# A four-layer image kernel: the row spectrum of the third layer stored component, frequency, line

## The chip, the cores and the metric

The kernel runs on one core of one Trainium2 chip. The metric is the device time of one execution in microseconds (us). The kernel before took 8232.35 us, the median of 3 runs (8224.83 to 8241.54). The profile shown below is of one more execution, whose span is 8232.3 us.

## The reference

Four images of 64 x 64 pixels and 128 channels pass through four residual layers, x = x + layer(groupnorm(x)), all in float32. The change lies in the third, a Fourier attention layer in which each of the 128 channels is one token, an image of 64 lines by 64 columns. Cut to what the changed code computes:

```python
# _L2_conv_ref: 128 tokens per image, 16 heads
tokens_norm = instance_norm(tokens)
k, q = fno_layer(tokens_norm, ..., (32, 32)), fno_layer(tokens_norm, ..., (32, 32))
v    = fno_layer(tokens_norm, ..., (64, 64))
attn = softmax(q @ k.T / scale) @ v                    # over the tokens, per head
attn = instance_norm(fno_layer(attn, proj_w, ...) + tokens)
m = gelu(fno_layer(instance_norm(attn), mixer_w1, ..., norm=...))
m = fno_layer(m, mixer_w2, ..., norm=...)
out = instance_norm(m) + attn

# fno_layer: resampled 1x1 convolution + spectral_conv, which is
xft = rfftn(x); out_ft[low modes] = xft[low modes] * w; irfftn(out_ft)
```

The layer has one channel in and one out per token, so a spectral weight is one complex number per mode. The Gram product of all tokens over their low modes stands for the scores of the convolution with a scalar part.

## The kernel before

The layers run one after the other. The first is a selective scan and takes most of the span; the third begins at about 6600 us and ends at about 7660 us of the profile; the fourth, windowed attention, takes the rest.

The third layer is `layer2_image`, a generator that is run once for each of the four images. `layer2` lets two images run interleaved: `Pace` keeps a model clock of each engine and `in_turn` advances the image that is due next, so the order of the instructions on TensorE (PE), VectorE (DVE), ScalarE (ACT) and GpSimd (POOL) is fixed when the program is built, and each engine works its list off in that order. All instructions are recorded in `Pace`'s helper, so the profile gives line L884 for nearly all of the layer; they are told apart by the names of their tiles. Images 0 and 1 form the first pair, 2 and 3 the second.

An image lies in SBUF as 32 tiles of 128 partitions, each tile holding two lines of the token images. The parts that the change or the prediction touches, in the order of an image:

- `token_stats` and the norm: DVE statistics `in_st`, matmuls `in_pm`, the scale `n_sc` on ACT and DVE, the selectors `so`, matmuls `pc`.
- `dft_y` transforms each line of 64 columns into 32 frequencies of two components. Eight groups of four matmuls write `pu` in PSUM (4 tiles of 128 values: line, component, frequency), and one ACT copy for each group brings 8 lines into `U`, which is `[128, 64 lines, 2 components, 32 frequencies]`. `dft_y` is called three times per image: once at the start on `xg`, and once in each of the two calls of `spectral`.
- The column transform of the first call, matmuls `px`: for each of 32 frequencies and 2 components, the 64 lines of one frequency are the stationary operand, `U[:, :, q, 4 * g + e]`, and the 68 columns of `quad` are moved. Four frequencies share a PSUM tile and are copied by ACT into `Xs`. GpSimd copies corners of `Xs` into `XG`, whose transposes are `pT`.
- The Gram product: `pv` (stationary `gram`, moved `U` for 8, 7 or 1 frequencies by 64 lines) goes by an ACT copy into a tile `V`, and then for each frequency a matmul `pG` takes the 66 x 64 slice `V_last[0][:, :, e]` as its stationary and as its moving operand.
- After `pT`, DVE copies `TT` and DVE and GpSimd build the three-part `Z`; the scores `psc` need it. Softmax on DVE and ACT (`Sc`), transposes `pp`, the combined matrix `BI`, and matmuls `pk`, whose result goes to HBM and back (`ti`, `z`).
- `pz`: for both images of the pair, products `WX` on DVE and GpSimd are the stationary operand, 68 contiguous columns, and 64 contiguous columns of `PT` are moved; ACT copies the result into `Zp`.
- `synthesis` (matmuls `pa`, `pb`), norms, and twice `spectral`: there four matmul groups `pq` move `U` for 16 lines by 32 frequencies over stationary `quad`, and DVE multiplies each result by `mix` into `Zp`.

The PSUM pool has three buffers for each of the tags `a` (`pu`, `pv`, `pT`) and `b` (`px`, `pq`, `pz`). A float32 matmul appears in the profile as two records.

Of the kernel before, what the change touches and what calls it, by code (L numbers as in the profile page):

```python
# [11 lines left out]
F32 = mybir.dt.float32  # L12
AF = mybir.ActivationFunctionType
ALU = mybir.AluOpType
# [3 lines left out]
P = 128  # L18
Q = 68
# [64 lines left out]
def layer0(sh, A, x_in, x_out, scr):  # L84
# [7 lines left out]
    with ExitStack() as ctx:  # L92
# [300 lines left out]
        def products(G, q, hT):  # L393
            U = G["unit"]
            rev = U["rev"]
            qo = 3 - q if rev else q
            e = qo // 2
            if U["yT"][e] is None:
                U["yT"][e] = psy.tile([P, 2, 2 * P], F32, name=f"yT{e}")
                if U["k"] == 0:  # L400
                    for r in range(2):
                        for s in range(2):
                            t0 = (2 * e + r) * P
                            nc.tensor.matmul(
                                U["yT"][e][:, r, s * P : (s + 1) * P],
                                lhsT=U["u"][:, s, t0 : t0 + P],
                                rhs=D_diag[:, s, :],
                                start=(r == 0 and s == 0),
                                stop=False,
                                skip_group_check=True,  # L410
                            )
                    U["started"] |= {(e, j) for j in range(4)}
            for j in range(4):
                jo = 3 - j if rev else j
                nc.tensor.matmul(  # L415
                    U["yT"][e][32 * jo : 32 * jo + 32, qo % 2, :],
                    lhsT=U["Ws"][G["g"]][:, :, 4 * q + j],
                    rhs=hT[:, j, :],
                    start=((e, jo) not in U["started"]),
                    stop=(G["g"] == 3),  # L420
                    skip_group_check=True,
                )
                U["started"].add((e, jo))
            if G["g"] == 3 and q % 2:

                y, k = U["y"], U["k"]
                ye = y[:, 2 * e : 2 * e + 2, :]
                if k == 1:
                    nc.scalar.copy(ye, U["yT"][e])
                else:  # L430
                    nc.vector.tensor_tensor(ye, ye, U["yT"][e], ALU.add)  # L431
                if k == 2:
                    for r in range(2):
                        nc.vector.bn_stats(U["st"][:, 4 * U["pc"] + 2 * e + r, 0, :], y[:, 2 * e + r, :])
                if q == 3:
                    nc.sync.dma_start(U["dst"](k), y)
# [482 lines left out]
def layer2_image(sh, w, pools, x_in, x_out, scr, wt, parity, beside):  # L919
# [4 lines left out]
    nc = sh.nc  # L924
    big, tmp, small, ps = pools
# [3 lines left out]
    tt, ts = nc.vector.tensor_tensor, nc.vector.tensor_scalar  # L929
# [3 lines left out]
    large = lambda name, shape=T: big.tile(shape, F32, name=name, tag="big", bufs=7)  # L933
# [53 lines left out]

    def dft_y(src):

        U = large("U2", [P, 64, 2, 32])  # L990
        for g in range(NJ // 4):
            pu = ps.tile([P, 4, P], F32, name="pu", tag="a")
            for q in range(4):
                nc.tensor.matmul(pu[:, q, :], lhsT=src[:, 4 * g + q, :], rhs=w["an"], start=True, stop=True)
            nc.scalar.copy(U[:, 8 * g : 8 * g + 8].rearrange("p t q r -> p (t q r)"), pu.rearrange("p q m -> p (q m)"))
            yield g == 7
        return U

    def synthesis(Z, put):


        def columns(g0):
            S = tmp.tile([P, 4, 2, P], F32, name="S2", bufs=3)
            for e in range(0, 4, 2):
                pa = ps.tile([P, 2, 256], F32, name="pa", tag="a")
                for q in range(2):
                    g = g0 + e + q
                    nc.tensor.matmul(
                        pa[:, q, :],
                        lhsT=Z[:, 4 * g : 4 * g + 4, :].rearrange("p t r -> p (t r)"),  # L1010
                        rhs=w["sy"],
                        start=True,
                        stop=True,
                    )
                nc.scalar.copy(S[:, e : e + 2].rearrange("p g q c -> p (g q c)"), pa.rearrange("p g m -> p (g m)"))
            return S

        S = columns(0)
        yield False
        for g0 in range(0, 16, 4):  # L1020
            S_next = columns(g0 + 4) if g0 < 12 else None
            for u in range(2):
                pb = ps.tile([P, 4, DM], F32, name="pb", tag="b")
                for q in range(2):
                    nc.tensor.matmul(
                        pb,
                        lhsT=w["bd"][64 * u : 64 * u + 64, q, :],
                        rhs=S[64 * u : 64 * u + 64, :, q, :],
                        start=(q == 0),
                        stop=(q == 1),  # L1030
                    )
                put(u, g0, pb)
            S = S_next
            yield g0 == 12

    def at(t, u, g0):
        return t.rearrange("p (g u) c -> p u g c", u=2)[:, u, g0 : g0 + 4, :]
# [47 lines left out]
    for n in range(2):  # L1085
        nc.tensor.matmul(
            pc[:, n : n + 1],
            lhsT=M2[:, n].rearrange("p a j u -> p (a j u)"),
            rhs=w["ones"][:, 0:1],
            start=True,  # L1090
            stop=True,
# [10 lines left out]
    U = yield from dft_y(xg)  # L1102
    Xs = own([P, 32, Q], "Xs", tmp)
    for g in range(8):
        px = ps.tile([64, 4, Q], F32, name="px", tag="b")
        for e in range(4):
            for q in range(2):
                nc.tensor.matmul(
                    px[:, e, :], lhsT=U[:, :, q, 4 * g + e], rhs=w["quad"][:, q, :], start=(q == 0), stop=(q == 1)
                )  # L1110
        nc.scalar.activation(Xs[0:64, 4 * g : 4 * g + 4, :], px, AF.Copy, scale=scT[:64])
        if g == 0:
            dc = Xs[0:64, 0, 0:Q:51]
            tt(dc, dc, sfT[:64].to_broadcast([64, 2]), ALU.add)
        if g % 4 == 3:
            nc.sync.dma_start(Xs[64:128, 4 * g - 12 : 4 * g + 4, :], Xs[0:64, 4 * g - 12 : 4 * g + 4, :])
        yield False
# [16 lines left out]
    V_last = None  # L1134
    for v, r0, r1 in ((1, 0, 8), (2, 8, 9), (0, 9, 16), (3, 16, 17), (0, 17, 24), (1, 24, 32), (None, 0, 0)):
        nr = r1 - r0
        if nr:
            V = tmp.tile([66, 64, 8], F32, name="V2", tag="S2", bufs=3)
            pv = ps.tile([66, 64, nr], F32, name="pv", tag="a")
            for q in range(2):  # L1140
                nc.tensor.matmul(pv, lhsT=w["gram"][:, v, q, :], rhs=U[:, :, q, r0:r1], start=(q == 0), stop=(q == 1))
            nc.scalar.copy(V[:, :, :nr], pv)
        if V_last is not None:
            for e in range(V_last[1]):
                Ve = V_last[0][:, :, e]
                nc.tensor.matmul(pG, lhsT=Ve, rhs=Ve, start=(n_done == 0), stop=(n_done == 31))
                n_done += 1
        V_last = V, nr
        yield False
# [29 lines left out]
    for h in range(8):  # L1179
        for a in range(2):  # L1180
            for n, r in enumerate((0, 1, 4)):
                nc.tensor.matmul(
                    psc[64 * a : 64 * a + 64, h, :],
                    lhsT=Z[:, n, 8 * a + h, :],
                    rhs=TT[:, r, :],
                    start=(n == 0),
                    stop=(n == 2),
# [66 lines left out]
    else:  # L1254

        for g in range(4):
            pzs = [ps.tile([Q, 8, 64], F32, name="pz", tag="b") for _ in beside]
            for e in range(8):
                r = 8 * g + e
# [43 lines left out]
    def spectral(src, mix):  # L1303
        U = yield from dft_y(src)
        Zm = own([Q, 64, 32], "Zp", tmp)
        for g in range(4):
            px = ps.tile([Q, 16, 32], F32, name="pq", tag="b")
            for q in range(2):
                nc.tensor.matmul(
                    px, lhsT=w["quad"][:, q, :], rhs=U[:, 16 * g : 16 * g + 16, q, :], start=(q == 0), stop=(q == 1)  # L1310
                )
            tt(Zm[:, 16 * g : 16 * g + 16, :], px, mix.unsqueeze(1).to_broadcast([Q, 16, 32]), ALU.mult)
            yield g == 3
        sp = large("sp")
        yield from synthesis(Zm, lambda u, g0, p: nc.scalar.copy(at(sp, u, g0), p))
        return sp


    m = large("m")
# [86 lines left out]
def layer3(sh, A, x_in, out, v_pads):  # L1406
# [5 lines left out]
    with ExitStack() as ctx:  # L1412
# [89 lines left out]
        def queries(b, by):  # L1502
# [12 lines left out]
            )  # L1515
            V = tmp.tile([98, 8, 2, P], F32, name="V3", bufs=3)
            for bx in range(8):
                for half in range(2):
                    r0 = 8 * by + 7 * half
                    nc.sync.dma_start(V[:, bx, half, :], v_pads[b % 2][r0 : r0 + 7, 8 * bx : 8 * bx + 14, :])  # L1520
            return q, V

# [27 lines left out]
        with tc.manual_schedule(engines=engines):  # L1550
# [3 lines left out]
            for s in range(NU + 6):  # L1554
# [19 lines left out]
                if s < NU:  # L1574
                    q, V = rows[s // 4]
                    ps = psS.tile([P, 2, CH], F32, name="ps3")
# [267 lines left out]
```

## Time and profile before

| | |
|---|---|
| median of 3 runs | 8232.35 us (8224.83 to 8241.54) |
| span of the profiled execution | 8232.3 us, 141196 instructions |
| busy over the span | PE 80%, DVE 82%, ACT 75%, POOL 67% |
| 6600 to 6757 us (first pair, up to `pk`) | PE 116.62, DVE 77.46, ACT 28.36, POOL 15.84 of 157 us |
| 7126 to 7278 us (the same of the second pair) | PE 113.27, DVE 82.39, ACT 38.94, POOL 15.98 of 152 us |

The shares over the whole span are those of the first layer above all. For the third layer the stages are read by themselves: in both stretches in the table PE is busy about three quarters of the time, and the other engines half of it or less. Three views are used below: groups of instructions by line with shapes kept apart (busy us, mean ns of one, idle time of the engine before them and who ended it), the chain of waits (start, length, engine and tile of each piece of the chain that ended last), and the timeline.

### The profile page before, as it was taken

To read this page: it belongs to the slowest core of one execution; us is meant where nothing else is said; L and a number is where in the kernel's file an instruction comes from. 1 tells how busy PE (TensorE), PEld (TensorE's weight loads), DVE (VectorE), ACT (ScalarE), POOL (GpSimd) and SP (SyncE) were. 2 spreads that over 40 slices of the span, in tenths; PEclk is the share of its full clock that TensorE was granted. 3 is DMA by queue.
4 is the path that set the end of the run, shared out by engine and by line. 5 is a ranking of instruction groups with operands and counts; after the bars stand their busy time and mean duration, and the time that the engine had idled before them with its cause. 6 is when DMAs were issued, how large, how long until landed. Compare 5 with 4: busy or idle time off the path is not lost.

```text
span 8232.3 us, 141196 instructions
## 1 busy us (share of the span) xinstructions
PE 6551.1 (80%) x52976; PEld 4166.6 (51%) x52976; DVE 6752.2 (82%) x7948; ACT 6192.0 (75%) x9798; POOL 5481.8 (67%) x2502
## 2 busy tenths in 40 slices
PE   7788888778888777888887777787778978587689
PEld 3344454444445444444544444454457756474456
DVE  2889999998999999889999999999944554635778
ACT  3899999988898898989988999999822222414567
POOL 0889899998888898888888999999900011020233
PEclk9899999999999999999999999999989989798799
DMA  6445555545555554555555445555541132330332
GB/s 122 158 146 185 162 170 176 162 158 153 183 168 173 179 171 156 159 169 168 173 177 178 163 154 178 177 176 177 174 92 47 25 97 64 83 106 20 108 94 79
DMA packets 1403839, 1165.69 MB, mean 142 GB/s; under 512 B 759829, under 2 KB 1197681, under 8 KB 1336210
## 3 DMA queue, kind: packets, MB, share of 16 engines
q1 hardware_dynamic: 1401474, 1154.93, 45.5%
q8 instruction: 417, 6.83, 0.3%
q14 instruction: 268, 2.20, 0.1%
q10 hardware_dynamic: 1680, 1.74, 0.1%
HBM read 962.66 MB, written 189.74 MB: 140 GB/s over the span
## 4 chain that ended last, share of the span: by engine, by line
PE 21%; DVE 11%; ACT 10%; issue 3%; DMA 2%; POOL 2%; SPq 1%; ACTq 0%; DVEq 0%; POOLq 0%
DVE h L493 5%; ACT hT L390 4%; ACT dA L492 3%; PE pt L380 2%; POOL dB L486 1%; PE po L696 1%; PE pf L691 1%; PE pz L884 1%; PE pt L1527 1%; PE pu L884 1%; DVE in_st L884 1%; PE pb L884 1%; DVE m L884 1%; PE pa L884 1%; PE ps L1581 1%
## 5 line engine op out<-in xcount | busy, mean ns | idle before, releaser
L493 DVE TENSOR_TENSOR_SCAN h<-dA,state,dB 128x512 f32<-128x512 f32 x4096 | 4960.2, 1271 | 340.3 <-ACT dA L492 211.7
L486 POOL TENSOR_TENSOR dB<-du,Bb 128x1024 f32<-128x1024 f32 x2048 | 4816.7, 2386 | 524.5 <-DVE h L493 381.6
L380 PE MATMUL pt<-ident,h 128*128 128x128 f32 x16384 | 2245.1, 281 | 993.4 <-ACT hT L390 988.5
L492 ACT ACTIVATE dA<-delta,A_neg 128x512 f32<-128x512 f32 x4096 | 2746.0, 690 | 166.3 <-DVE h L493 139.4
L380 PEld LDWEIGHTS pt<-ident,h 128*128 128x128 f32 x16384 | 1836.1, 142 | 2029.6 <-ACT hT L390 1783.0
L390 ACT COPY hT<-pt 128x1024 f32<-128x1024 f32 x2048 | 2068.8, 1010 | 187.3 <-PE pt L380 170.8
L415 PE MATMUL yT<-hT,W 128*32 128x256 f32 x16384 | 1394.7, 413 | 2.7 <-DVE y L431 2.1
L884 POOL COPY XG<-Xs 64x9 f32<-64x9 f32 (+2 forms) x44 | 10.9, 293 | 1016.6 <-ACT Xs L884 1016.5
L415 PEld LDWEIGHTS yT<-hT,W 128*32 128x32 f32 x16384 | 454.1, 150 | 350.9 <-issue 333.8
L215 PE MATMUL cv<-xn,taps 128*128 128x512 f32 x1152 | 613.3, 633 | 0.0
L1565 POOL TENSOR_TENSOR S<-S,sm 128x784 f32<-128x784 f32 x128 | 191.1, 1493 | 432.4 <-DVE sm L1563 248.4
L326 PE MATMUL dp<-xd,w_dt 65*128 65x512 f32 x512 | 296.2, 661 | 106.1 <-ACT Ct L313 92.5
L335 POOL TENSOR_TENSOR du<-delta,u 128x1024 f32<-128x1024 f32 x128 | 304.9, 2382 | 66.1 <-DVE delta L332 66.1
L215 PEld LDWEIGHTS cv<-xn,taps 128*128 128x128 f32 x1152 | 183.5, 188 | 234.4 <-issue 233.0
L307 PE MATMUL xd_ps<-u,w_x 128*48 128x512 f32 x512 | 251.1, 614 | 41.3 <-DMA u<-l_xw 16.2
L1572 ACT ACTIVATE S<-S,mx 128x196 f32<-128x196 f32 x512 | 227.9, 448 | 34.8 <-DVE mx L1599 34.2
L692 ACT ACTIVATE h<-pf,b 128x512 f32<-128x512 f32 x128 | 88.0, 687 | 146.6 <-PE pf L691 146.6
L332 DVE SCALAR_TENSOR_TENSOR delta<-delta,dp 128x512 f32<-128x512 f32 x256 | 169.5, 662 | 24.2 <-ACT delta L330 24.2
L326 PEld LDWEIGHTS dp<-xd,w_dt 65*128 65x128 f32 x512 | 78.2, 192 | 218.4 <-ACT Ct L313 151.1
L329 ACT ACTIVATE delta<-dp 128x512 f32<-128x512 f32 x256 | 152.4, 595 | 24.2 <-PE dp L326 19.3
L330 ACT ACTIVATE delta<-delta 128x512 f32<-128x512 f32 x256 | 162.4, 635 | 8.1
L1527 PE MATMUL pt<-ident,S 128*98 128x128 f32 x1024 | 165.3, 286 | 3.3 <-POOL S L1565 1.9
(344 smaller groups left out, 6929.3 us busy)
## 6 DMA issues: line engine op xcount, KB each, us to landing
Bb<-l_B SPq DMA_DIRECT2D x512, 1024.0 KB
W<-l_W SPq DMA_DIRECT2D x512, 256.0 KB
l_y<-y SPq DMA_DIRECT2D x128, 512.0 KB
u<-l_xw SPq DMA_DIRECT2D x64, 512.0 KB
y<-l_y SPq DMA_DIRECT2D x64, 512.0 KB
u<-l_xr SPq DMA_DIRECT2D x64, 512.0 KB
V<-l_v SPq DMA_DIRECT2D x512, 49.0 KB
wr<-wt SPq DMA_DIRECT2D x128, 136.0 KB
```

The lines of the kernel that those rows point to most:

```text
L215: nc.tensor.matmul(pm, lhsT=taps[:, s, t, :], rhs=xn[:, dy : dy + 8, dx : dx + 64], start=(t == 0), stop=(t == 8),)
L307: nc.tensor.matmul(xd_ps, lhsT=w_x[:, s, k, :], rhs=u[:, s, :], start=(s == 0), stop=(s == 1))
L326: nc.tensor.matmul(dp, lhsT=w_dt[:, k, s * P : (s + 1) * P], rhs=xd, start=True, stop=True)
L335: nc.gpsimd.tensor_tensor(du, delta, u, ALU.mult)
L380: nc.tensor.transpose(pt[:, j, s, :], G["h"][:, s, t0 : t0 + 32, :].rearrange("p t n -> p (t n)"), sh.ident)
L390: return lambda: nc.scalar.copy(hT, pt.rearrange("p j s d -> p j (s d)"))
L415: nc.tensor.matmul(U["yT"][e][32 * jo : 32 * jo + 32, qo % 2, :], lhsT=U["Ws"][G["g"]][:, :, 4 * q + j], rhs=hT[:, j, :], start=((e, jo) n ...
L486: nc.gpsimd.tensor_tensor(dB, du, B_now[:, q : q + 1, :].to_broadcast([P, 2, CH]), ALU.mult)
L492: nc.scalar.activation(dA, delta[:, s, :], AF.Exp, scale=A_neg[:, k, s, n : n + 1])
L493: nc.vector.tensor_tensor_scan(h[:, s, :, q], dA, dB[:, s, :], state[:, s, n : n + 1], ALU.mult, ALU.add)
L884: r = f(*args, **kw)
L1527: nc.tensor.transpose(pt[:, half, hp, :], U["S"][:, e, hp, 98 * half : 98 * half + 98], sh.ident)
```

## The change

`U` becomes `[128, 2 components, 32 frequencies, 64 lines]`, and `V` `[66, 8 frequencies, 64 lines]`. The loops, the number of instructions and their order on every engine stay as they are; what changes is the order of the elements that they read and write.

```diff
-        U = large("U2", [P, 64, 2, 32])
+        U = large("U2", [P, 2, 32, 64])
...
-            nc.scalar.copy(U[:, 8 * g : 8 * g + 8].rearrange("p t q r -> p (t q r)"), pu.rearrange("p q m -> p (q m)"))
+            nc.scalar.copy(
+                U.rearrange("p q r t -> p (q r) t")[:, :, 8 * g : 8 * g + 8],
+                pu.rearrange("p j m -> p (j m)").rearrange("p (t k) -> p k t", t=8),
+            )
...
-                    px[:, e, :], lhsT=U[:, :, q, 4 * g + e], rhs=w["quad"][:, q, :], start=(q == 0), stop=(q == 1)
+                    px[:, e, :], lhsT=U[:, q, 4 * g + e, :], rhs=w["quad"][:, q, :], start=(q == 0), stop=(q == 1)
...
-            V = tmp.tile([66, 64, 8], F32, name="V2", tag="S2", bufs=3)
-            pv = ps.tile([66, 64, nr], F32, name="pv", tag="a")
+            V = tmp.tile([66, 8, 64], F32, name="V2", tag="S2", bufs=3)
+            pv = ps.tile([66, nr, 64], F32, name="pv", tag="a")
...
-                nc.tensor.matmul(pv, lhsT=w["gram"][:, v, q, :], rhs=U[:, :, q, r0:r1], start=(q == 0), stop=(q == 1))
-            nc.scalar.copy(V[:, :, :nr], pv)
+                nc.tensor.matmul(pv, lhsT=w["gram"][:, v, q, :], rhs=U[:, q, r0:r1, :], start=(q == 0), stop=(q == 1))
+            nc.scalar.copy(V[:, :nr, :], pv)
...
-                Ve = V_last[0][:, :, e]
+                Ve = V_last[0][:, e, :]
...
-            px = ps.tile([Q, 16, 32], F32, name="pq", tag="b")
+            px = ps.tile([Q, 32, 16], F32, name="pq", tag="b")
...
-                    px, lhsT=w["quad"][:, q, :], rhs=U[:, 16 * g : 16 * g + 16, q, :], start=(q == 0), stop=(q == 1)
+                    px, lhsT=w["quad"][:, q, :], rhs=U[:, q, :, 16 * g : 16 * g + 16], start=(q == 0), stop=(q == 1)
...
-            tt(Zm[:, 16 * g : 16 * g + 16, :], px, mix.unsqueeze(1).to_broadcast([Q, 16, 32]), ALU.mult)
+            tt(
+                Zm[:, 16 * g : 16 * g + 16, :],
+                px.rearrange("p r t -> p t r"),
+                mix.unsqueeze(1).to_broadcast([Q, 16, 32]),
+                ALU.mult,
+            )
```

## The prediction, made before the changed kernel ran

> **What bounds the kernel now.** The change touches only the third layer, so I first asked the chain of waits for that layer alone, 6600 to 7660 us (first column start, second length, then engine and tile). There TensorE's `px` holds 5.3% of 1060 us, 56 us, and `pG` 2.9%, 31 us. The records say the same: 512 of `px` and 256 of `pG`. So nearly every one of them lies on the chain. These pieces give the pace of one record:
>
> ```profile
> 6717.90 10.84 PE px L884 x96
> ...
> 6730.96 0.57 PE pv L884 x4
> 6731.53 2.10 PE pG L884 x16
> 6733.63 2.97 PE psc L884 x96
> ...
> 7213.10 1.72 PE pv L884 x4
> 7214.82 0.89 PE pu L884 x8
> 7215.71 0.44 PE pv L884 x4
> ...
> 7238.07 12.61 PE px L884 x112
> ```
>
> A `px` record takes 10.84/96 = 113 ns, though it moves only 68 columns. The `pu` records, 128 columns over contiguous weights, take 0.89/8 = 111 ns, and the 512-column `pv` 1.72/4 = 430 ns, 0.84 ns a column; 68 columns should then take 57 ns. `pG` takes 2.10/16 = 131 ns here and 3.79/30 = 126 ns in another piece, with 64 columns. `pz`, which has 68 contiguous weight columns and moves 64, takes 15.03/240 = 62.6 ns in its piece of the chain at 6841 us. What `px` and `pG` have in common is a strided stationary operand. The groups by line show it too (after the bar: busy us, mean ns of one record with its pipeline):
>
> ```profile
> L884 PEld LDWEIGHTS pz<-PT,WX 128*68 128x68 f32 x2048 | 132.8, 147 | 22.0 <-DVE WX L884 18.4 <-POOL WX L884 2.5 <-issue 1.1
> ...
> L684 DVE TENSOR_TENSOR hT<-hT,ph 128x512 f32<-128x512 f32 x32 | 37.6, 1261 | 13.0 <-PE ph L671 13.0
> ...
> L884 PEld LDWEIGHTS px<-quad,U 128*64 128x64 f32 x512 | 57.9, 206 | 2.2 <-ACT U L884 1.7
> L884 ACT COPY U<-pu 128x512 f32<-128x512 f32 x96 | 55.5, 584 | 77.7 <-PE pu L884 74.7 <-DMA Xs<-Xs 2.8
> ...
> L884 PEld LDWEIGHTS pG<-V 66*64 66x64 f32 x256 | 32.5, 216 | 11.2 <-issue 10.7 <-ACT V L884 0.3
> ...
> L884 DVE TENSOR_TENSOR Zp<-pq,mix 68x512 f32<-68x512 f32 x32 | 21.6, 684 | 53.3 <-PE pq L884 53.3
> ...
> L884 ACT COPY Zp<-pz 68x512 f32<-68x512 f32 x16 | 9.3, 581 | 143.9 <-PE pz L884 143.9
> ```
>
> A load of 64 columns at a stride takes 206 and 216 ns, one of 68 contiguous columns 147 ns. Last I looked in the timeline for what stands next behind PE. DVE's and GpSimd's building of `Z` runs while PE does `px`:
>
> ```profile
> 6717.93 0.49 DVE L884 COPY TT<-pT 128x320 f32<-128x320 f32 x1 [3.85 <-PE pT L884]
> ...
> 6731.00 1.25 DVE L884 TENSOR_TENSOR Z<-Z 128x1024 f32<-128x1024 f32 x1
> ```
>
> It takes 6717.93 to 6732.25, 14.3 us, and `psc`, at 6733.45 in the timeline, needs its result: only 1.2 us of slack.
>
> [...]
>
> **The change part by part.** No instruction is added, removed or moved on any queue, DMA queues included, and no wait is added; sizes and buffers stay.
>
> *`px`.* The weights become 64 contiguous columns. By `pz` I take 63 ns: 512 x (113 - 63) = 25.6 us of PE time. Bounds: 57 ns (the moving side) and 113.
>
> *`pG`.* Both operands become contiguous, 126 to 62 ns: 256 x 64 ns = 16.4 us.
>
> *`pv`.* The single-frequency ones (32 records) go from 110 (0.44/4) to about 60 ns: 1.6 us. The others moved runs of 8 or 7 floats at 430 and 375 ns, the same 0.84 ns a column as anything else: nothing.
>
> *`pq`.* Runs of 16 floats in place of 32. `pq` now takes 1.72/4 = 430 ns, exactly like `pv` with runs of 8; 16 lies between: nothing.
>
> *ACT `U` copy.* Reads PSUM at a stride of 64 floats in runs of 8, writes runs of 8. `Zp<-pz` has the same pattern, 64 by 8, strided PSUM read and runs of 8 written, at 581 ns against the 584 of the present `U` copy. I take nothing. Bounds: 0 and, if it went like DVE's strided `hT`, 1261/690 (the latter for a contiguous operation of that size), 1.8 times, 1070 ns. Up to 890 ns, the length of a `pu` group, PE hides it.
>
> *ACT `V` copy.* The same 448 or 512 elements, now contiguous on both sides; 0.53 to 0.58 us before, nothing.
>
> *DVE `Zp<-pq`.* Reads PSUM at a stride of 16 floats. The trace has no DVE read of PSUM at a stride. Lower bound 0 (a gain is excluded, the access is contiguous now), by ACT's strided PSUM read; upper bound 577 ns, by `hT` (1261 - 684), which strides in SBUF on both sides. I take 0, since ACT's read at a wider stride is free. Of 32, PE hides those in the first `spectral` (DVE waits 1.9 us for PE before most). In the second, DVE is the chain for three `Zp` in a row at 7025 us, and two more stand before `in_d` and `q`: five per pair, ten in all, so 0 to 5.8 us.
>
> The gross gain is 25.6 + 16.4 + 1.6 = 43.6 us, 21.8 per pair. What of it lands, walking each pair's chain:
>
> 1. `px` of the first image (128 records, 6.4 us). First pair: the other image's `in_st`, `in_pm`, `n_sc` and `so` come between; PE will wait about 0.5 and 0.8 us for DVE; 5.1 lands. Second pair: all 32 `in_st` run from 7194.67 to 7200.92 while PE does 80 `px`. They start after the first `px` group, so they move up only 0.8 us, and `in_pm` with them; then two groups of 0.8 land: 2.5 in all.
> 2. `pG` and `pv` of the first image among `pu`: PE-bound, 4.5 lands in each.
> 3. `px` of the second image before `pT`: 32 and 16 records, 1.6 and 0.8.
> 4. From `pT` to `psc`: 6.0 us saved in the first pair (96 `px`, 16 `pG`, one `pv`), 6.8 in the second (112 `px`). But `Z` still takes 14.3 us. Only the slack lands: 1.1 and, with `psc` at 7255.40 and `Z` done at 7252.41, 2.9.
> 5. `pG` during the softmax, 1.2 us: PE waits there for DVE anyway, nothing.
> 6. The last 32 `pG`, before the second `pT`, 2.0 in each.
>
> Sum: 5.1 + 4.5 + 1.6 + 1.1 + 2.0 = 14.3 and 2.5 + 4.5 + 0.8 + 2.9 + 2.0 = 12.7, together 27.0 us. What follows (`pk`, the trip through HBM, `pz`, `synthesis`, the fourth layer) hangs on these in order and moves up with them. The new PE waits of 3 to 5 us cost a little clock: the same `psc` records take 4.31/92 = 47 ns behind a wait (at 6769 us) and 2.97/96 = 31 otherwise, and a 448-column `pv` at 6747 us 2.57/4 = 643 ns against 375. I take 2 us off: 25. The profiled span, 8232.3, is the median of the runs, so 8207 us. About 0.2%, 16 us, is what a measurement of this kernel can tell from no change; the runs before spread by 17.
>
> **The rivals.**
>
> *Main case, PE's loads halve and `Z` and `in_st` swallow part:* 18 to 35 us, 8197 to 8214. Chance 0.60.
>
> *The whole gross gain lands,* because waits that I charge are shorter than they look: 36 to 44 us, 8188 to 8196. Against it: `Z`'s 14.3 us stand in both pairs. Chance 0.12.
>
> *Swallowed:* `Zp` at 1261 ns takes 5.8 us, the clock after new waits 5, and little more than parts 2 and 6 of the walk lands (13 us): 8216 to 8232. Chance 0.21. Here also belongs the case that the weight load does not get faster because it was bound by something else, so that `px` stays at 113 ns; against it speaks `pz`.
>
> *Slower: ACT's `U` copy becomes the bound.* Place: the 12 runs of `dft_y`, 96 copies. PE makes a `pu` group in 890 ns. It costs from there on, and eats the gain of 27 us at 890 + 27000/96 = 1170 ns, twice today's; at 1300 ns it costs 96 x 0.41 = 39, net 12 us slower, 8244. `Zp<-pz` at 581 ns speaks against it. Chance 0.07.
>
> **How the numbers follow.** 8207 is the main case. The range runs from the whole gain, 8188, over the swallowed gain down to 6 us, 8226. Faster by over 0.2% means under 8215.9: main case and whole gain, 0.72; within 0.2% 0.21; slower 0.07.
>
> **What would show it.** Right: `px` records at 60 to 65 ns, `pG` near 62; loads near 140 ns; `U` copy at 580, `pq` at 430; in the chain, DVE and POOL `Z` in the place of `px` before `psc`. Wrong: `px` still over 100; `U` copy over 890; `Zp<-pq` over 1000 and in the chain; or `psc` not waiting for `Z`.

## The result, and the profile after

The changed kernel took 8211.02 us (median of 16 runs, 8198.43 to 8223.07), the kernel before 8234.63 (16 runs, the three named above among them): ratio 0.9973, 95% interval 0.9965 to 0.998, or 22 us less (16 to 29). The prediction was 8207, 25 us less. The profiled execution has a span of 8217.7 us, which is on the slow side of its own runs; so stages are compared below, not spans. The third layer's first `pu` begins anywhere from 6648 to 6669 us in the profiles of this document, though nothing ahead of it was changed; much of the scatter of a single execution thus arises before the changed code.

The groups by line of the changed kernel, for the rows that were shown of before:

```profile
L884 ACT COPY U<-pu 128x512 f32<-128x512 f32 x96 | 55.6, 584 | 70.9 <-PE pu L884 70.6
...
L884 PEld LDWEIGHTS px<-quad,U 128*64 128x64 f32 x512 | 33.8, 146 | 2.2 <-ACT U L884 1.7
...
L884 DVE TENSOR_TENSOR Zp<-pq,mix 68x512 f32<-68x512 f32 x32 | 21.6, 685 | 54.2 <-PE pq L884 54.2
...
L884 PEld LDWEIGHTS pG<-V 66*64 66x64 f32 x256 | 16.6, 137 | 11.1 <-issue 10.1 <-ACT V L884 0.3
```

The loads fell from 206 and 216 ns to 146 and 137. The copy into `U` and the product `Zp`, the two operations that the change gave strides, stayed at 584 and 685. In the chain of waits the pace of the records follows:

```profile
6699.72 0.24 PE pv L884 x4
...
6714.46 1.24 DVE Z L884
6715.76 2.83 POOL Z L884
6718.61 1.24 DVE Z L884
6719.91 2.82 POOL Z L884
...
6725.22 4.97 PE psc L884 x92
...
6742.16 1.89 PE pG L884 x30
```

`pG` takes 1.89/30 = 63 ns (126 before), the one-frequency `pv` 0.24/4 = 60 (110), and a piece of 48 `px` at 7222.46 us 3.00 us, 62.5 ns (113). In the short `pv` only the moving operand changed its order: with single floats 256 bytes apart it took 1.8 times as long (110 against 60 ns). In `px` it is the stationary operand alone, at the same stride and 1.8 times too (113 against 62.5). Why the stride costs this is not shown. In `pG` both changed, and which of the two set its pace was not separated. Between `pT` and `psc`, where `px` filled the chain before, now stand `Z` on GpSimd and VectorE by turns. (In the second pair the chain names a DMA for one of the links; `Z` takes 14.3 us there too.) And `psc` itself takes 54 ns a record behind that wait, at a granted clock of 0.56, where it took 31 ns at 1.00.

The stages, each from the first record of its matmuls to the first of the next, in us, first and second pair:

| stage | before | after | saved | predicted |
|---|---|---|---|---|
| first `px` to the `pu` after `pc` (part 1) | 17.2, 17.6 | 11.4, 18.0 | 5.8, -0.5 | 5.1, 2.5 |
| that `pu` to the first `pT` (2 and 3) | 27.7, 27.7 | 21.4, 20.7 | 6.3, 7.0 | 6.1, 5.3 |
| first to second `pT` (4 to 6) | 36.3, 36.8 | 33.7, 34.0 | 2.6, 2.9 | 3.1, 4.9 |
| sum | | | 14.7, 9.4 | 14.3, 12.7 |

So these stages gained 24.1 us, against 27.0 less 2 for the clock. The rest of the layer was 4.7 us longer in this profile (1006.8 to 987.4 in all); 4.6 of it lie behind the second pair's first `pk`, and the next section shows that this was scatter for the greater part.

### The profile page after: what moved, and what is told of

Its sections match the earlier page's. It is cut to its first block, busy times and chain, and to the rows that moved or that the text cites. A ratio compares the mean times of both kernels' runs of the same rounds, so it can differ in the third digit from the quotient of the medians.

```text
span 8217.7 us, 141198 instructions
## 1 busy us (share of the span) xinstructions
PE 6518.3 (79%) x52976; PEld 4132.6 (50%) x52976; DVE 6753.0 (82%) x7948; ACT 6192.3 (75%) x9798; POOL 5483.6 (67%) x2502
## 4 chain that ended last, share of the span: by engine, by line
PE 20%; DVE 11%; ACT 11%; issue 3%; DMA 2%; POOL 2%; SPq 1%; DVEq 0%; ACTq 0%; POOLq 0%
DVE h L493 5%; ACT hT L390 4%; ACT dA L492 4%; PE pt L380 1%; POOL dB L486 1%; PE po L696 1%; PE pf L691 1%; PE pt L1535 1%; DVE in_st L884 1%; PE pu L884 1%; PE pb L884 1%; PE pa L884 1%; DVE m L884 1%; PE pz L884 1%; PE ps L1589 1%
## 5 line engine op out<-in xcount | busy, mean ns | idle before, releaser
L1580 ACT ACTIVATE S<-S,mx 128x196 f32<-128x196 f32 x512 | 227.9, 448 | 34.2 <-DVE mx L1607 33.5
```

## The experiments

Each was timed in 5 rounds beside the kernel before. The numbers of stages come from the profile of each, which is one execution.

**The two halves of the change.** First `U` alone: the change without its Gram part.

```diff
-            V = tmp.tile([66, 8, 64], F32, name="V2", tag="S2", bufs=3)
+            V = tmp.tile([66, 64, 8], F32, name="V2", tag="S2", bufs=3)
-            nc.scalar.copy(V[:, :nr, :], pv)
+            nc.scalar.copy(V[:, :, :nr], pv.rearrange("p r t -> p t r"))
-                Ve = V_last[0][:, e, :]
+                Ve = V_last[0][:, :, e]
```

> U in the new order, V and its Gram slices in the old one. Theory (two separate gains, each a strided PE operand): px at 63 ns, pG still at 126. First pair: 7 us less between the first px and the first pT (44.9 before), second pair 3 us less (45.3); between the two pT of a pair 1 to 3 us less; in all about 14 us less than before. Rival (most of the gain is the Gram's): less than 5 us. Rival (px not bound by its weights): px stays at 113 ns and nothing is gained.

Then `V` alone, from the kernel before: `V` as `[66, 8, 64]`, its copy reading `pv.rearrange("p t r -> p r t")`, `Ve` as in the change.

> U in the old order, V and its Gram slices in the new one. Theory: pG from 126 to 62 ns, px still at 113. From the first px to the first pT 4.5 us less in each pair, between the two pT 3 us less, in all about 15 us less than before; together with the px-only kernel a little more than the whole change, since both share the slack before psc. Rival (pG bound by its moving operand or its wait for V): pG over 100 ns, less than 4 us in all.

`U` alone: 0.9979 (0.9973 to 0.9986), 17 us less. `px` 62 ns, `pG` still at 3.79/30 = 126. From first `px` to first `pT` 37.0 and 43.0 us (44.9 and 45.3 before), between the `pT` 35.4 and 35.6. `V` alone: 0.9978 (0.9970 to 0.9987), 18 us less; `pG` at 63 ns, 40.6 and 39.4 us to the first `pT`, then 31.8 and 33.6. Each half is worth about what the walk gave it (14 and 15 had been expected), and the sum of the two, 35, is more than the whole. The profiles say the same: the layer took 14.7 us less with `U` alone, 18.1 with `V` alone, and 18.5 to 22.2 with both. That fits the slack before `psc`, which the halves share; the kernels with a short `Z`, below, test it. `V` alone even has the shorter way between the two `pT`, since there the slow `px` keep TensorE busy while `Z` is built, and `psc` then runs at 31 ns:

```profile
6709.01 0.46 PE pT L884 x5
...
6724.15 2.97 PE psc L884 x96
...
6738.94 1.89 PE pG L884 x30
```

**ScalarE's runs of eight.** The copy into `U` with the same data, but in the order of the tile `pu`:

```diff
-                U.rearrange("p q r t -> p (q r) t")[:, :, 8 * g : 8 * g + 8],
-                pu.rearrange("p j m -> p (j m)").rearrange("p (t k) -> p k t", t=8),
+                U.rearrange("p q r t -> p t (q r)")[:, 8 * g : 8 * g + 8, :],
+                pu.rearrange("p j m -> p (j m)").rearrange("p (t k) -> p t k", t=8),
```

> As the changed kernel, but ScalarE writes U in single floats 256 bytes apart (reading PSUM contiguously) instead of in runs of eight. Theory (ScalarE pays nothing for a stride on either side): the U copy stays at 584 ns and the time is that of the changed kernel within 5 us. Rival ([...]the runs of eight are what keeps the copy cheap): the copy takes 900 to 1100 ns, more than a pu group of 890, and the 96 copies cost up to 20 us, which takes most of the gain back.

The stated theory fell at once:

```profile
L884 ACT COPY U<-pu 128x512 f32<-128x512 f32 x96 | 92.8, 1056 | 48.9 <-PE pu L884 48.6
```

Single floats written 256 bytes apart take 1056 ns, 1.8 times the 584 of the runs of eight. The time did not follow: 0.9973 (0.9963 to 0.9982), as the changed kernel. The copy is now longer than a `pu` group of 890 ns, but in the first `dft_y` of a pair that does not show: from the first `pu` to the first `px` it took 10.5 and 10.4 us, against 9.6 to 10.1 and 9.5 to 10.8 in three profiles of the changed kernel. TensorE's granted clock is low there at first (0.50 from 6667.75 to 6671.50 us of the changed kernel, 0.55 from 7173.93 to 7177.00), and the 64 `pu` of the first pair take 9.08 us, over 1.1 us a group, which by an estimate from these figures would hide the copy. In the second `spectral`, though, ScalarE is on the chain itself, and each longer copy counts: from the first copy into `U` there to the ninth it takes 27.5 us in both pairs, against 25.3 in all three profiles. So some 4 us of loss are in the trace, of the up to 20 expected, and the times can't tell them.

**The changed kernel again,** twice, without any edit.

> The changed kernel itself, beside the others. Theory: 22 to 25 us less than before; first pu to first pu of the next pair 506 us (520.6 before); in the second pair, from the first pk to the end of the layer, either again 4 us longer than before (then the change costs something there) or the same within 2 us (then the 4 us of the first profile were scatter).

> The changed kernel once more, on the chip of the one with the extra matmuls: 20 to 25 us less than before; from the first px of the second pair to the pu after pc 17.5 to 18.5 us again, with the px groups after in_pm at 2.0 us each.

0.9968 (0.9956 to 0.9981) and 0.9971 (0.9959 to 0.9983), so 26 and 24 us less. The third layer took 988.3 and 984.6 us; from the first `pu` to that of the next pair it was 508.6 and 506.0 (506 expected, 520.6 before). From its first `pk` to the end of the layer the second pair had been 4.6 us longer than before in the first profile (395.8 against 391.2); here it is 392.5 and 393.2, 1.3 and 2.0 longer. So most of that loss was scatter. The first part of the second pair was slow each time, 18.6 and 17.6 us (17.6 before), with the two `px` groups at 2.0 us each.

**Does `Z` swallow the gain?** In both orders the second products, their sums and the bias of `Z` were left out, so `Z` is only its first product; `Pace` is charged as before, so that no instruction of the rest changes its place.

```diff
-        nc.gpsimd.tensor_tensor(
-            zt, TT[:, t2 : t2 + 1, :].to_broadcast(H), w["W2"][:, n, :].unsqueeze(2).to_broadcast(H), ALU.mult
-        )
+        nc.spend("gpsimd", "tensor_tensor", zt)
...
-            tt(Zn, Zn, w["Wb"].unsqueeze(2).to_broadcast(H), ALU.add)
+            nc.spend("vector", "tensor_tensor", Zn)
...
-        tt(Zn, Zn, zt, ALU.add)
+        nc.spend("vector", "tensor_tensor", Zn)
```

> The kernel before without the second products of Z, their sums and the bias (GpSimd's products and two DVE operations for each of the three parts; Z is then its first product only). Theory (Z bounds psc only after the change): little faster than before for the first image of a pair, 1 to 3 us from the first to the second pT of each pair, plus what the second image's Z was worth: 2 to 10 us in all.

> The changed kernel with the same parts of Z left out. Theory (Z swallowed 4 to 5 us in each pair): against the short-Z kernel in the old order the change is now worth 32 to 36 us instead of 22 to 25; from the first to the second pT it saves 8 to 9 us in each pair, where with the whole Z it saved 2.6 and 2.9. Rival (the gain was lost elsewhere, to ScalarE or the clock): the difference stays at 22 to 25 us and psc still waits.

In the old order 0.9995 (0.9987 to 1.0002): `Z` was worth nothing that can be told. In the new order 0.9948 (0.9934 to 0.9962). Their difference is 0.0047, 39 us (26 to 52 by the two intervals), of a gross gain of 43.6; the stages of the table, added up, give 37. Between the two `pT` the old order takes 36.9 and 37.6 us, no less than with the whole `Z` (1 to 3 us had been expected), the new one 26.9 and 27.7: 10 us saved in each pair, where with the whole `Z` it was under 3. The chain of the new order has no `Z` and no wait before `psc`:

```profile
6690.45 0.46 PE pT L884 x5
...
6700.47 2.97 PE psc L884 x96
...
6715.42 1.89 PE pG L884 x30
6717.31 0.47 PE pT L884 x5
```

**The clock after the new waits.** Sixteen matmuls before `psc` keep TensorE busy while `Z` is built:

```diff
+    for _ in range(16):
+        nc.nc.tensor.matmul(
+            psc[:, 0:2, :].rearrange("p h s -> p (h s)"), lhsT=sh.ident, rhs=sh.ident, start=True, stop=True
+        )
```

> The changed kernel with 16 matmuls of 128 by 128 (about 3.6 us of TensorE) put before psc into psc's own bank, which psc then overwrites; nothing is left out. Theory (the new wait for Z lets the clock fall): the first psc of a pair goes from 52 to about 31 ns a record, and the stretch from the first to the second pT is 1 to 3 us shorter than in the changed kernel in each pair. Rival (the slow psc has another cause): psc stays over 45 ns and the stretch gets no shorter or up to 3 us longer.

Then, besides, thirteen of 64 columns before `in_pm` of the fourth image, in the same way:

> The changed kernel with the 16 matmuls before psc, and with 13 more of 128 by 64 (about 2.9 us of TensorE) before the fourth image's in_pm, in the in_pm bank, which in_pm then overwrites; nothing is left out. Theory (in the second pair the wait for in_st halved the clock, and that took the 2.5 us which the faster px should have brought there): from the first px of the second pair to the pu after pc 18.0 us become 15 to 16, the two px groups there 1.0 instead of 2.0 us each. Rival (another cause): it stays at 17.5 or more. In all 26 to 30 us less than before.

With the sixteen, 0.9965 (0.9953 to 0.9977); the first `psc` takes 3.02 us for 92 records, 33 ns, and the way between the two `pT` 32.8 and 31.8 us (33.5 to 33.8 and 33.0 to 34.0 in three profiles of the changed kernel). With both, 0.9961 (0.9948 to 0.9973). Between the two `pT` this kernel takes 32.7 and 33.1 us, so in the second pair the shorter way did not come again. In the second pair's first part:

```profile
7178.37 6.19 DVE in_st L884 x32
...
7184.60 1.09 PE in_pm L884 x8
7185.68 1.09 PE px L884 x16
7186.77 0.56 PE in_pm L884 x4
7187.34 1.10 PE px L884 x16
```

The same pieces of the changed kernel:

```profile
7185.11 6.20 DVE in_st L884 x32
...
7191.35 1.92 PE in_pm L884 x8
7193.27 2.00 PE px L884 x16
7195.27 0.99 PE in_pm L884 x4
7196.27 2.02 PE px L884 x16
```

`in_st` takes as long (6.19 against 6.20 us) and holds `in_pm` as before; only what TensorE does afterwards nearly halves, 1.09 and 1.10 us for 16 `px` against 2.00 and 2.02. The stretch from `px` to `pu` is 15.0 us, against 17.6 to 18.6 in the three profiles of the changed kernel: 2.6 us less than the 17.6 of before, where 2.5 had been predicted.

**A shorter `Z`.** Its second products in three buffers, two in the spent image tile, so that GpSimd runs ahead; the sums come last.

```diff
+    zts = [Z[:, 3]] + [xg[:, 8 * n : 8 * n + 8].rearrange("p a b -> p (a b)").rearrange("p (h s) -> p h s", s=64) for n in (0, 1)]
...
-        tt(Zn, Zn, zt, ALU.add)
+        if n == 2:
+            for q in range(3):
+                tt(Z[:, q], Z[:, q], zts[q], ALU.add)
```

> The changed kernel with Z's second products in three buffers (two of them in the spent image tile xg), so that GpSimd makes all three without waiting for VectorE, and the three sums after the last first product; nothing is left out, and an instruction or two of the other image changes places. Theory (after the change Z's chain of GpSimd and VectorE by turns sets the time between the two pT): it shrinks from 14.3 to about 10 us, the stretch between the pT by 3 to 5 us in each pair, and the kernel is 28 to 34 us faster than before. Rival (GpSimd and VectorE slow each other when they run side by side): Z takes over 13 us and the stretch shrinks by less than 1 us.

> The same with the 16 matmuls before psc too. Theory: with Z at 10 us TensorE hardly waits, so they now stand in the way: the stretch between the two pT is 0 to 3 us longer than in the kernel with Z ahead alone. Rival (the clock falls there too): 1 to 2 us shorter.

0.9963 (0.9951 to 0.9975), and with the matmuls before `psc` 0.9966 (0.9954 to 0.9979). The theory failed for `Z`: from `TT` to its last sum it takes 13.8 us, not 10. This is VectorE and GpSimd in the timeline:

```profile
6697.09 5.20 POOL L884 TENSOR_TENSOR Z<-TT,W 128x1024 f32<-128x1024 f32 x1 [20.40 <-DVE TT L884]
...
6700.56 2.81 DVE L884 TENSOR_TENSOR Z<-Z,Wb 128x1024 f32<-128x1024 f32 x1
...
6702.26 5.72 POOL L884 TENSOR_TENSOR xg<-TT,W 128x1024 f32<-128x1024 f32 x2
...
6703.30 2.92 DVE L884 TENSOR_TENSOR Z<-Z 128x1024 f32<-128x1024 f32 x1
```

GpSimd's first product takes 5.20 us instead of 2.9, and VectorE's sum 2.92 instead of 1.2, as the rival had it; the last section takes these numbers apart. Still the stretch between the two `pT` fell to 26.2 us in the first pair (33.7), and to 32.9 in the second: in this kernel the planner puts `psc` behind one more `pv` and `pG` group of the other image, so TensorE has work in the wait. How much is the new place and how much the 0.5 us off `Z` was not taken apart. With the matmuls too the stretch takes 28.0 and 31.6 us: in the first pair, where TensorE hardly waits, they stand in the way for 1.8 us, as the theory said, and in the second it is 1.3 us shorter.

No version can be told from the changed kernel by its time: the intervals of 0.9961, 0.9963, 0.9965, 0.9968, 0.9971 and 0.9973 overlap. By the profiles the layer took 978.7 us with both sets of matmuls, 982.7 with the sixteen alone, 984.3 and 982.7 with `Z` ahead without and with them, and 990.9 with ScalarE's single floats, against 984.6 to 988.3 for the changed kernel.

## Why the prediction was right

*The sizes of the operations.* `px` was put at 63 ns and measured 62.5, `pG` at 62 and measured 63, the short `pv` 60 and 60, the `U` copy 584 and 584, `Zp<-pq` 684 and 685. That the nearest rows, `pz` for the weights and `Zp<-pz` for the copy, had the same pattern of bytes is the likely reason why these were exact. `Zp<-pq` had no such row: it was put at 684 by another engine's read, and that it held was partly luck. The gross gain of 43.6 us is borne out too, within the error: 39 us land once `Z` is out of the way.

*What lands.* Parts 2 and 3 came as walked in the first pair (6.3 for 6.1) and with 1.7 us more in the second, by the clock, as shown below. In parts 4 to 6 `Z` became the bound before `psc`, as said; the short-`Z` pair of kernels shows this as cause and not as coincidence.

*The term that was mis-sized: the clock.* "I take 2 us off" was too little, and the walk counted none of it where it fell. The prediction's own figures, 47 and 31 ns for `psc`, make 1.5 us for each of the two first `psc` alone. The first `psc` of each pair lost 2 us (4.97 and 5.05 after, at a granted clock of 0.56 and 0.55; 2.97 in both before, at 1.00). In the second pair TensorE waited 3.2 us for `in_st` and then ran at half the clock (0.50 from 7191.35 to 7198.29 us); the windows of this stretch, before and after, show it in the column PEclk, which follows the five engines' busy times:

```profile
7192.00:7209.50 17.50, 17.10 (x146) 16.73 (x147) 8.36 (x43) 4.03 (x9) 0.85 (x5) 1.00 0.08 17
```

```profile
7183.00:7201.20 18.20, 14.43 (x146) 13.83 (x147) 8.37 (x43) 4.17 (x10) 0.76 (x4) 0.72 0.07 16
```

From 1.00 to 0.72, while TensorE's busy time in the stretch fell from 17.1 to 14.4 us: part 1 of the second pair brought -0.5 instead of 2.5. The extra matmuls gave it back (15.0 us in place of 18.0), so the cause is shown. (At a clock of 0.50 the 16 contiguous `px` of a group took 2.00 us, 125 ns each, no less than the 1.92 us of the strided ones before, at 1.00.) That makes some 7 us of clock where 2 were charged.

A part of it is no new loss. The kernel before had paid for the clock too, in places where this profile of the changed kernel did not. The `pu` behind `pc` in the second pair, before (granted clock 0.55) and after (1.00):

```profile
7209.78 3.31 PE pu L884 x16
```

```profile
7201.39 1.84 PE pu L884 x16
```

These 1.5 us are most of the 1.7 by which parts 2 and 3 there were better than walked; in the changed kernel's second profile the same `pu` took 3.21 us, and those parts 22.1 us instead of 20.7. A `pv` in the first pair's softmax also went from 2.57 us, at a clock of 0.73, to 1.86, at 1.00. So the clock cost about 5 us net, 3 more than charged, and the kernel with both sets of matmuls agrees: its parts save 29.0 us against 24.1. In this profile the waits ahead of the slow `px` and of the two slow `psc` were 3.2 us (`in_st`), 4.6 and 3.8 us (`Z`). All in all the parts came to 24.1 us. That this lies within 1 us of the 25 of the prediction is partly luck: the walk was about 2 us too low elsewhere, 0.7 of it in part 1 of the first pair, the rest in small pieces.

*The rivals.* The whole gain did not land, mostly because of `Z`. `Zp` did not slow down, so that loss fell away. ScalarE did not become the bound with runs of eight. With single floats its copy would have taken 1056 ns, close to the upper bound of 1070 and short of the 1170 from which the change was to lose; even that cost only the 4 us of the second `spectral`. So "up to 890 ns PE hides it" was not the right bound: in the first `dft_y`, where 64 `pu` took 9.08 us at a clock of 0.50 at first, a group lasted over 1.1 us, and in the second `spectral`, where ScalarE is on the chain, the copies were not hidden (27.5 us for the stretch against 25.3).

## What to carry to other kernels

Here it paid to lay a tensor out for TensorE, which reads it many times: 768 records that read single floats at a stride as their stationary operand took 1.8 to 2.0 times as long (`px` 113 against 62.5 ns; `pG`, whose moving operand had the stride too, 126 against 63), 32 short `pv` with such a moving operand 110 against 60 ns, while the 96 copies that write the new order, in runs of 32 bytes, cost nothing (584 ns before and after). Before counting such a gain, walk the chain and ask at each wait what the faster engine will meet: here under three fifths of 43.6 us landed, mostly because another chain of 14.3 us was only 1.2 us behind in the first pair and 3 us in the second. And the faster TensorE also waited longer here, 3.2 to 4.6 us, and paid for it in its clock, 0.50 to 0.56 behind these waits.

## What the runs showed of the hardware that was not expected

- ScalarE paid for single floats written 256 bytes apart (1056 ns for 128 x 512) and not for runs of eight floats (584), nor for reading PSUM at a stride of 256 bytes (584 before and after). VectorE's read of PSUM at 64 bytes cost nothing either (685 against 684).
- VectorE and GpSimd slowed each other where their operations on `Z` ran side by side. GpSimd's product of 128 x 1024 took 1.90 us where no VectorE operation of that size ran beside it, 2.82 beside one VectorE product of 1.22, and 5.20 beside three that took 3.48: 1.6 to 1.9 us and the whole of VectorE's time. VectorE's sums, 1.22 us alone, took 2.80 to 2.92 when they began during such a product: each ended 1.1 us after it. By an estimate from these figures some 4 of the 14.3 us of `Z`, in both orders, are this slowing: 0.9 for each of three products and 1.1 at the last sum. From the changed kernel:

```profile
6745.12 1.90 POOL L884 TENSOR_TENSOR Z<-TT,W 128x1024 f32<-128x1024 f32 x1 [18.76 <-DVE TT L884]
```

- A wait of some 3 us on TensorE (3.2 in the changed kernel), filled with matmuls whose result is thrown away, made the following `px` records 1.8 times as fast (1.09 against 2.00 us for 16).
- The clock fell without a wait. In the kernel before, TensorE was busy with strided `px` and `pG` for the whole of one window, and had half the clock in the next (first column after the comma PE, then as above; PEclk 1.00 and 0.50):

```profile
6711.00:6714.40 3.40, 3.40 (x32) 3.40 (x31) 0.15 (x1) 0.48 (x1) 0.00 (x0) 1.00 0.00 0
6714.40:6717.80 3.40, 3.40 (x29) 3.18 (x28) 0.00 (x0) 0.48 (x1) 0.00 (x0) 0.50 0.00 0
```

The same came at 7236.7 us (PEclk 0.50 up to 7240.0); in the changed kernel PEclk is 1.00 at these places (6706.0 to 6716.6 and 7218.0 to 7229.1 us). Why is not shown. The strided `px` did not feel it: the 96 from 6717.90, the first 3.3 us of them at half the clock, took 113 ns each, and 80 at the full clock from 7192.00 took 114.
